# Two scores and two weighted sums by turns: changing the order of attention matmuls in a two-layer kernel

## The chip, the cores and the metric

The kernel runs on one NeuronCore of a Trainium2 chip. The metric is device time in microseconds (us) of one execution. Before the change it is 3041.32 us, the median of three runs (3039.63 to 3041.74). One further execution was recorded by the hardware profiler; its span is 3042.2 us. Engine names are those of the profile: PE is the matmul engine (PEld its weight loads), ACT the scalar engine (exponentials, copies), DVE the vector engine, POOL the GpSimd engine, SP the engine that issues most DMAs. A trailing q (ACTq, SPq) is the queue on which an engine issues DMAs.

## The reference, cut to what matters

The input is `x` of shape (8, 512, 32, 32): eight images, 512 channels, 1024 positions. Two layers follow each other.

```python
# layer 0: 8 heads of 64 channels
h   = group_norm(xf, gn_w, gn_b)
qkv = einsum('oc,bct->bot', qkv_w, h) + qkv_b
q, k, v = split(qkv per head)
q, k, v = fake_quant(q), fake_quant(k), fake_quant(v)   # range over ALL images: a barrier
w   = softmax(einsum('bct,bcs->bts', q*scale, k*scale))
a   = einsum('bts,bcs->bct', w, v)
x   = xf + einsum('oc,bct->bot', proj_w, a) + proj_b
# layer 1: one head of 512 channels
h   = group_norm(x)
q, k, v = h@wq + bq, h@wk + bk, h@wv + bv
x   = x + (softmax(q k^T / sqrt(512)) v) @ wp + bp
```

`fake_quant` takes one minimum and maximum over all images, so all of q, k and v must be computed before any attention of layer 0 may begin. Layer 1's softmax is over one head with 512 channels; its matrices can be combined ("folded") ahead of time: wq with wk into `wa`, wv with wp into `wm`, and the biases likewise.

## The kernel before

It has two phases. Phase 1 (to about 700 us in the profile) normalizes, computes q, k, v of all images and writes them to device memory. Phase 2 runs layer 0's attention for one image while layer 1 works on the image before it. All matmuls pass through one helper, `mm` (line 93), which fixes their order on PE to the order in which the program emits them; other engines' instructions may be put in another order by the framework.

**Attention** is a Python generator over units. A unit is one step of 128 keys for a pair of heads and 512 queries: image b, pair j, half hf, step s; 8 x 4 x 2 x 8 = 512 units. A *burst* is one step of the generator and handles four units; eight units make a *group* (b, j, hf), which is finished by its row sums.

```python
def pair_ps(name):  return ps_s.tile([P, 2, 512], F32, tag="s")   # 2 buffers of two PSUM banks: st
def av_bank(name):  return ps_v.tile([P, 512], F32, tag="v")      # 2 buffers: av
def bank(name):     return ps_o.tile([P, 512], F32, tag="o")      # 2 buffers: everything else

def scores(u):                       # bf16, contraction over 64: both heads of the pair
    st = pair_ps(...)
    for i, r in enumerate(HALF):
        mm(st[:, i, :], lhsT=kt[r, bass.ts(s, P)], rhs=qt[r, bass.ts(hf, 512)], ...)
    pt = ptp.tile([P, 2, 512], F32, tag="p")        # 6 buffers
    nc.scalar.activation(pt, st, AF.Exp, scale=esc)
    ...                                             # s >= 1: DVE adds pt to acc (row sums)

def weighted(u):                     # fp32, two heads side by side in the output's partitions
    if s == 0:
        avs[b, j, hf] = av_bank(...)
    for i, r in enumerate(HALF):
        mm(avs[b, j, hf][r, :], lhsT=pairs[b, j][2][:, s, r], rhs=pt[:, i, :], ...)

def finish(b, j, hf):
    sm = bank(...)
    for i, r in enumerate(HALF):
        mm(sm[r, :], lhsT=ones[:, 0:CH], rhs=acc[:, i, :], start=True, stop=True)
    rs = accp.tile([P, 512], F32, tag="rs")
    nc.scalar.copy(rs, sm)
    inverse(rs, 2, n * 8, rs_d[n], nm)              # 1 / row sums, via device memory
    ao[b, j, hf] = aop.tile([P, 512], F32, tag="ao")
    nc.vector.scalar_tensor_tensor(ao[b, j, hf], avs.pop((b, j, hf)), scl[:, 2:3], rs, ALU.mult, ALU.mult)

for u in range(0, len(units), 4):    # one burst
    ...                              # at hf == 0 and s == 4: load_pair of the next pair
    more = u + 4 < len(units)
    if more:
        scores(u + 4); scores(u + 5)
    for v in range(u, u + 4):
        weighted(v)
    if s == 0 and u > 0:
        finish(*units[u - NT][:3])
    if more:
        scores(u + 6); scores(u + 7)
    yield 6.0 + (s == 0), b
```

When two bursts follow each other with nothing between them, the last two scores of the one and the first two of the next make four scores in a row. `inverse` spreads a row of sums over partitions, takes the reciprocal and broadcasts it back:

```python
def inverse(rs, n_rows, at, scratch, nm):
    k = 4 * n_rows
    group = P // n_rows
    s8 = small.tile([P, 8], F32, tag="s8")[:, 0:k]
    for i in range(n_rows):
        nc.scalar.dma_start(s8[i * group : (i + 1) * group, :],
                            rs[i * group : i * group + 1, :].rearrange("o (p k) -> o p k", k=k))
    r8 = rcs[:, at : at + k]
    nc.vector.reciprocal(r8, s8)
    nc.sync.dma_start(scratch.rearrange("r (p k) -> (r p) k", k=k), r8)
    for i in range(n_rows):
        nc.sync.dma_start(rs[i * group : (i + 1) * group, :],
                          scratch[i : i + 1, :].partition_broadcast(group))
```

**Other work** (fold, projection `pj`, layer 1's `g`, `v2ps`, `s`, `o`) is cut into pieces of four fp32 matmuls (`yield 4.0`; each appears as two instructions in the profile) and interleaved with the bursts by a counter:

```python
F_FIRST = 8.0
folded = 0.0
for w in fold():                     # 8 pieces of 4 matmuls, then 2 bias sums of 8 matmuls each
    folded += w
    while pos < (folded - F_FIRST) * A_IMAGE / F_FOLD:
        advance()                    # one burst
while done < 1:                      # the rest of the first image: burst after burst
    advance()
...
def layer1(b, xt, steps):            # steps: the group norm, in three parts
    for gap, _ in zip(GN_GAPS, steps):   # GN_GAPS = (6.0, 3.0, 3.0)
        yield -gap                   # attention bursts, until gap is filled
```

The group norm makes two tiny matmuls (`gps`, 4 columns); around them, in each of the three gaps, one burst is run.

Of the kernel before, what the change touches and what calls it, by code (L numbers as in the profile page):

```python
# [16 lines left out]
P = 128  # L17
B, C, HH, WW = 8, 512, 32, 32
T = HH * WW
CC = C // P  # L20
NT = T // P
# [25 lines left out]
def attn_pair_kernel(  # L47
# [51 lines left out]
    def norm_steps(src, dst, wcol, bank, nm):  # L99

        st = small.tile([P, CC, NH, 6], F32, tag="gst", name=f"gst_{nm}")
        mv = small.tile([P, CC, 2], F32, tag="gmv", name=f"gmv_{nm}")
        for cc in range(CC):
            for hf in range(NH):
                nc.vector.bn_stats(st[:, cc, hf, :], src(cc, hf))
            nc.vector.bn_aggr(mv[:, cc, :], st[:, cc, :, :].rearrange("p a s -> p (a s)"))
        yield
        ps = bank(f"gps_{nm}")
        mm(ps[:, 0:CC], lhsT=gavg, rhs=mv[:, :, 0], start=True, stop=True)
        mean = small.tile([P, CC], F32, tag="gmean", name=f"gmean_{nm}")  # L110
        nc.vector.tensor_copy(mean, ps[:, 0:CC])  # L111

        d = small.tile([P, CC], F32, tag="gd", name=f"gd_{nm}")
        nc.vector.tensor_sub(d, mv[:, :, 0], mean)
        nc.vector.tensor_mul(d, d, d)
        nc.vector.tensor_add(d, d, mv[:, :, 1])
        yield
        ps2 = bank(f"gps2_{nm}")
        mm(ps2[:, 0:CC], lhsT=gavg, rhs=d, start=True, stop=True)
        rstd = small.tile([P, CC], F32, tag="grstd", name=f"grstd_{nm}")  # L120
        nc.vector.tensor_scalar(rstd, ps2[:, 0:CC], EPS, None, ALU.add)
        nc.gpsimd.tensor_tensor(rstd, rstd, mhalf, ALU.pow)
        nc.vector.tensor_mul(rstd, rstd, vec[:, wcol : wcol + CC])
        for hf in range(NH):
            for cc in range(CC):
                nc.vector.tensor_scalar(  # L126
                    dst(cc, hf), src(cc, hf), mean[:, cc : cc + 1], rstd[:, cc : cc + 1],
                    ALU.subtract, ALU.mult,
                )
        yield  # L130
# [20 lines left out]
    with ExitStack() as fast:  # L151
# [41 lines left out]
        def row_sums(ps, terms):  # L193


            n = len(terms) * CC
            for i, (w, wide) in enumerate(terms):
                for e in range(CC):
                    mm(
                        ps, lhsT=wide[:, e, :], rhs=w[:, e, :],  # L200
                        start=(i == 0 and e == 0), stop=(i * CC + e == n - 1),
                    )

        def widen(dst, col):
            for e in range(CC):
# [10 lines left out]
        with tc.tile_pool(name="p1w", bufs=1) as p1w, tc.tile_pool(name="p1", bufs=2) as p1, tc.tile_pool(  # L216
# [37 lines left out]
            def bias(i):  # L254

                ps = bank(f"bias{i}")
                row_sums(ps, ((wqkv[:, :, bass.ts(i, C)], gbb),))
                if i == 2:
                    nc.vector.tensor_add(vb, vb, ps)  # L259
                    return  # L260
                b4 = qkb[:, bass.ts(i, PAIRS)]
                by_channel(b4, ps)
                nc.vector.tensor_add(
                    b4, b4, vec[:, V_QKB + i * PAIRS : V_QKB + (i + 1) * PAIRS]
                )
# [102 lines left out]
        def inverse(rs, n_rows, at, scratch, nm):  # L368


            k = 4 * n_rows
            group = P // n_rows
            s8 = small.tile([P, 8], F32, tag="s8", name=f"s8_{nm}")[:, 0:k]
            for i in range(n_rows):
                nc.scalar.dma_start(  # L375
                    s8[i * group : (i + 1) * group, :],
                    rs[i * group : i * group + 1, :].rearrange("o (p k) -> o p k", k=k),
                )
            r8 = rcs[:, at : at + k]
            nc.vector.reciprocal(r8, s8)  # L380
            nc.sync.dma_start(scratch.rearrange("r (p k) -> (r p) k", k=k), r8)
            for i in range(n_rows):
                nc.sync.dma_start(
                    rs[i * group : (i + 1) * group, :],
                    scratch[i : i + 1, :].partition_broadcast(group),
                )
# [20 lines left out]
        def attention():  # L407

            units = [(b, j, hf, s) for b in range(B) for j in range(PAIRS) for hf in range(NH)
                     for s in range(NT)]
            pairs = {(0, 0): load_pair(0, 0)}
            pts, accs, avs, sums = {}, {}, {}, []

            def scores(u):
                b, j, hf, s = units[u]
                nm = f"{b}_{j}_{hf}"
                qt, kt, _ = pairs[b, j]  # L420
                st = pair_ps(f"st_{nm}_{s}")
                for i, r in enumerate(HALF):
                    mm(
                        st[:, i, :], lhsT=kt[r, bass.ts(s, P)],
                        rhs=qt[r, bass.ts(hf, 512)], start=True, stop=True,
                    )
                pt = ptp.tile([P, 2, 512], F32, tag="p", name=f"pt_{nm}_{s}")
                nc.scalar.activation(pt, st, AF.Exp, scale=esc)  # L428
                if s == 1:
                    accs[b, j, hf] = accp.tile([P, 2, 512], F32, tag="acc", name=f"acc_{nm}")  # L430
                    nc.vector.tensor_add(accs[b, j, hf], pts[u - 1], pt)
                elif s > 1:
                    nc.vector.tensor_add(accs[b, j, hf], accs[b, j, hf], pt)  # L433
                pts[u] = pt

            def weighted(u):
                b, j, hf, s = units[u]
                if s == 0:
                    avs[b, j, hf] = av_bank(f"av_{b}_{j}_{hf}")
                pt = pts.pop(u)  # L440
                for i, r in enumerate(HALF):
                    mm(
                        avs[b, j, hf][r, :], lhsT=pairs[b, j][2][:, s, r], rhs=pt[:, i, :],
                        start=(s == 0), stop=(s == NT - 1),
                    )

            def finish(b, j, hf):
                nm = f"{b}_{j}_{hf}"
                acc = accs.pop((b, j, hf))
                sm = bank(f"sm_{nm}")  # L450
                for i, r in enumerate(HALF):
                    mm(sm[r, :], lhsT=ones[:, 0:CH], rhs=acc[:, i, :], start=True, stop=True)
                rs = accp.tile([P, 512], F32, tag="rs", name=f"rs_{nm}")
                nc.scalar.copy(rs, sm)
                n = (b * PAIRS + j) * NH + hf
                inverse(rs, 2, n * 8, rs_d[n], nm)
                ao[b, j, hf] = aop.tile([P, 512], F32, tag="ao", name=f"ao_{nm}")
                nc.vector.scalar_tensor_tensor(  # L458
                    ao[b, j, hf], avs.pop((b, j, hf)), scl[:, 2:3], rs, ALU.mult, ALU.mult
                )  # L460

            scores(0)
            scores(1)
            yield 0.0, 0
            scores(2)
            scores(3)
            for u in range(0, len(units), 4):
                b, j, hf, s = units[u]
                if hf == 0 and s == 4:
                    n = b * PAIRS + j + 1  # L470
                    if n < B * PAIRS:
                        pairs[divmod(n, PAIRS)] = load_pair(*divmod(n, PAIRS))


                more = u + 4 < len(units)
                if more:
                    scores(u + 4)
                    scores(u + 5)
                for v in range(u, u + 4):
                    weighted(v)  # L480
                if s == 0 and u > 0:
                    finish(*units[u - NT][:3])
                if more:
                    scores(u + 6)
                    scores(u + 7)
                yield 6.0 + (s == 0), b
            finish(*units[-1][:3])
            yield 1.0, B
# [52 lines left out]
        def layer1(b, xt, steps):  # L541

            for gap, _ in zip(GN_GAPS, steps):
                yield -gap
            hn = hns.pop(b)
            nxt = ahead = None
            vt = l1p.tile([P, NT, C], F32, tag="v", name=f"v2_{b}")
# [76 lines left out]
        def fold():  # L626
# [14 lines left out]
                widen(wide[:, i], col)  # L641
            for i, (dst, w, w2) in enumerate(((gb, wa, wn[NK1]), (ob, wm, wn[WP1]))):
                ps = bank(f"fold_b{i}")
                row_sums(ps, ((w, wide[:, 0]), (w2, wide[:, 1 + i])))
                by_channel(dst, ps)
                yield 8.0
            nc.vector.tensor_add(ob, ob, vec[:, V_BP : V_BP + CC])

        def check_sums():
# [15 lines left out]
        A_IMAGE = PAIRS * NH * (NT * 1.5 + 1.0)  # L665
        F_IMAGE = 4.0 * (8 + 8 + 8 + 16 + 16)
        F_FOLD = 4.0 * (8 + 4)
        F_FIRST = 8.0
        pos, done = 0.0, 0

        def advance():
            nonlocal pos, done
# [18 lines left out]
                advance()  # L691
        while done < 1:
            advance()
        start, other = pos, 0.0
        for w in others():
            until = pos - w
# [369 lines left out]
```

## Time and profile before

| what | value |
|---|---|
| time, median of 3 | 3041.32 us |
| span of the profiled execution | 3042.2 us |
| mean granted PE clock | 0.994 |
| PE / DVE / ACT busy | 2971.1 / 1454.5 / 709.1 us |
| first score of the attention | 705.33 us |
| last piece of fold work ends | about 808 us |
| first projection piece | 856.47 us |

How to read it: busy times are sums over an engine's instructions, and idle time counts only on the engine that sets the end. A wait in the profile is named "engine, what it was about to do <- what released it". The granted clock is the share of full speed that PE's clock was given in a stretch; a mean below 1 means that some stretches ran at half speed, and in those PE counts as busy. Timeline lines give the start, the duration, the engine, line, operation, output <- input, count, and in brackets the idle time before it and its releaser. PE's `st` is a score, `av` a weighted sum, `sm` a row sum, `pt` the exponential of a score, `ao` the finished attention output.

### The profile page before, as it was taken

The page shows a single profiled execution, that of the slowest core. Times are in us where ns is not written, and L with a number is a line of the kernel's source. Part 1 is how long each engine was busy: PE and PEld are TensorE (multiplying, and loading weights), DVE is VectorE, ACT ScalarE, POOL GpSimd, SP SyncE. Part 2 cuts the span into 40 slices and gives each one's busy share as a digit, 9 for nine tenths or more (in the row PEclk, how much of TensorE's full clock was granted, in tenths as well). Part 3 has the DMA queues.
Part 4 walks back from the last instruction along what each step waited for, and adds up shares of the span by engine and source line. Part 5 has one row for each costly group of instructions (what it writes and reads, how often), then busy time and mean ns, then how long its engine had stood idle before and what let it go on. Part 6 is the DMA issues. An engine that isn't in the chain of part 4 may idle for free.

```text
span 3042.2 us, 22770 instructions
## 1 busy us (share of the span) xinstructions
PE 2971.1 (98%) x8664; PEld 1193.5 (39%) x8664; DVE 1454.5 (48%) x2017; ACT 709.1 (23%) x793; POOL 18.5 (1%) x28
## 2 busy tenths in 40 slices
PE   7999999999899999999999999999999999999999
PEld 3444444443233333433333333333333433333443
DVE  6555554447664446344534544364446345533311
ACT  0000000004542333232333223332333233232001
POOL 0000000000000000000000000000000000000000
PEclk9999999999999999999999999999999999999999
DMA  6222222113110111021101101110111012000000
GB/s 252 104 104 104 104 104 81 76 76 128 56 56 28 60 43 63 10 73 63 35 25 63 59 28 50 41 59 28 59 49 63 21 59 61 13 20 23 21 14 22
DMA packets 123287, 182.83 MB, mean 60 GB/s; under 512 B 32800, under 2 KB 65568, under 8 KB 122528
## 3 DMA queue, kind: packets, MB, share of 16 engines
q1 hardware_dynamic: 110336, 180.69, 17.2%
q10 hardware_dynamic: 12832, 0.59, 0.3%
q8 instruction: 70, 1.15, 0.2%
q14 instruction: 49, 0.40, 0.0%
HBM read 113.53 MB, written 67.40 MB: 59 GB/s over the span
## 4 chain that ended last, share of the span: by engine, by line
PE 96%; ACT 1%; issue 1%; DMA 1%; DVE 0%; ACTq 0%; SPq 0%; POOL 0%; POOLq 0%; DVEq 0%
PE av L93 16%; PE s L93 15%; PE o L93 15%; PE qkps L93 15%; PE pj L93 7%; PE g L93 7%; PE v2ps L93 7%; PE vps L93 7%; PE st L93 4%; PE sm L93 2%; ACT pt L428 1%; PE fold L93 1%; PE fold_b L93 0%; PE bias L93 0%; ACTq L375 0%
## 5 line engine op out<-in xcount | busy, mean ns | idle before, releaser
L428 ACT ACTIVATE pt<-st,esc 128x1024 f32<-128x1024 f32 x512 | 547.0, 1114 | 700.9 <-PE st L93 684.3
L433 DVE TENSOR_TENSOR acc<-acc,pt 128x1024 f32<-128x1024 f32 x384 | 469.6, 1223 | 252.5 <-ACT pt L428 233.9
L93 PE MATMUL av<-pt,v 128*64 128x512 f32 x2048 | 483.9, 616 | 3.1 <-DVE ao L458 3.1
L93 PE MATMUL o<-p,v 128*128 128x512 f32 x1024 | 452.4, 595 | 0.7 <-DVE gmean_b L111 0.7
L93 PE MATMUL s<-g,h 128*128 128x512 f32 x1024 | 450.3, 596 | 0.0
L93 PE MATMUL qkps<-h,wqkv 128*128 128x512 f32 x1024 | 447.2, 596 | 2.2 <-DVE h L126 2.2
L93 PEld LDWEIGHTS qkps<-h,wqkv 128*128 128x128 f32 x1024 | 194.4, 191 | 241.9 <-issue 235.9
L93 PEld LDWEIGHTS o<-p,v 128*128 128x128 f32 x1024 | 192.1, 190 | 243.7 <-issue 241.6
L93 PEld LDWEIGHTS s<-g,h 128*128 128x128 f32 x1024 | 191.7, 190 | 243.8 <-issue 243.0
L93 PEld LDWEIGHTS av<-pt,v 128*64 128x64 f32 x2048 | 139.4, 140 | 285.2 <-issue 279.4
L93 PE MATMUL pj<-ao,wp 128*128 128x512 f32 x512 | 225.1, 595 | 0.0
L93 PE MATMUL g<-h,wa 128*128 128x512 f32 x512 | 224.9, 595 | 0.0
L93 PE MATMUL v2ps<-wm,h 128*128 128x512 f32 x512 | 222.9, 593 | 0.0
L93 PE MATMUL vps<-wqkv,h 128*128 128x512 f32 x512 | 221.3, 592 | 0.8 <-DVE vb L259 0.8
L93 PE MATMUL st<-q,k 64*128 64x512 bf16 x1024 | 160.1, 382 | 42.5 <-ACT pt L428 42.5
L296 DVE TENSOR_SCALAR_CACHE_REDUCE qk<-qkps,qkb 128x1024 f32<-128x1024 f32 x64 | 82.2, 1284 | 217.4 <-PE qkps L93 217.3
L637 ACT COPY wa<-fold 128x512 f32<-128x512 f32 x4 | 2.3, 586 | 703.0 <-PE fold L93 703.0
L583 ACT ACTIVATE p<-s 128x512 f32<-128x512 f32 x128 | 76.5, 597 | 361.0 <-PE s L93 361.0
L571 DVE COPY v<-v2ps 128x512 f32<-128x512 f32 x64 | 43.9, 686 | 224.2 <-PE v2ps L93 224.2
L587 DVE TENSOR_TENSOR acc<-acc,p 128x512 f32<-128x512 f32 x96 | 66.2, 689 | 169.1 <-ACT p L583 168.8
L93 PEld LDWEIGHTS vps<-wqkv,h 128*128 128x128 f32 x512 | 97.2, 190 | 123.6 <-issue 122.0
L93 PEld LDWEIGHTS v2ps<-wm,h 128*128 128x128 f32 x512 | 96.7, 190 | 122.1 <-issue 122.1
(112 smaller groups left out, 1386.3 us busy)
## 6 DMA issues: line engine op xcount, KB each, us to landing
x<-in_x_dram SPq DMA_DIRECT2D x32, 512.0 KB, 5.4
q_d<-qk SPq DMA_DIRECT2D x32, 512.0 KB, 2.6
raw<-q_d SPq DMA_DIRECT2D x32, 512.0 KB, 3.4
k_d<-qk SPq DMA_DIRECT2D x32, 512.0 KB, 2.6
raw<-k_d SPq DMA_DIRECT2D x32, 512.0 KB, 4.3
v_d<-v SPq DMA_DIRECT2D x64, 256.0 KB, 2.0
raw<-v_d SPq DMA_DIRECT2D x32, 512.0 KB, 4.2
x<-in_x_dram SPq DMA_DIRECT2D x64, 256.0 KB, 2.6
```

The source lines that it names most:

```text
L93: ins = nc.tensor.matmul(*args, **kw).ins
L296: nc.vector.tensor_scalar(qk, ps.rearrange("p a n -> p (a n)"), qkb[:, t : t + 1], None, ALU.add, ALU.max, accum_out=mx[:, g : g + 1],)
L428: nc.scalar.activation(pt, st, AF.Exp, scale=esc)
L433: nc.vector.tensor_add(accs[b, j, hf], accs[b, j, hf], pt)
L571: nc.vector.tensor_copy(vt[:, t, :], ps)
L583: nc.scalar.activation(pt, ps, AF.Exp, scale=SM1)
L587: nc.vector.tensor_add(acc, acc, pt)
L637: nc.scalar.copy(dst[:, e, :], ps)
```

## The change

It has five parts. Where bursts follow each other (a new flag `dense`: from the start of folding to the end of the first image, and in the gaps of layer 1's group norm), a burst is emitted as two scores, two weighted sums, two scores, two weighted sums, with `finish` last. It is meant to give each exponential the time of two weighted sums before its buffer is needed again. The sums of the folded biases are emitted in pieces of four matmuls instead of eight, so that bursts can come between, and attention starts one piece later (`F_FIRST` 12). The row sums are spread by one DMA on SP's queue, which also carries the loads, instead of one per row on ACT's queue. In the group norm the difference from the mean is taken from PSUM directly, ahead of the copy of the mean.

```diff
@@ norm_steps
-        nc.vector.tensor_copy(mean, ps[:, 0:CC])
-        d = small.tile([P, CC], F32, tag="gd", name=f"gd_{nm}")
-        nc.vector.tensor_sub(d, mv[:, :, 0], mean)
+        d = small.tile([P, CC], F32, tag="gd", name=f"gd_{nm}")
+        nc.vector.tensor_sub(d, mv[:, :, 0], ps[:, 0:CC])
+        nc.vector.tensor_copy(mean, ps[:, 0:CC])
@@ row_sums: after each term's four matmuls
+                yield 4.0
@@ inverse
-            for i in range(n_rows):
-                nc.scalar.dma_start(
-                    s8[i * group : (i + 1) * group, :],
-                    rs[i * group : i * group + 1, :].rearrange("o (p k) -> o p k", k=k),
-                )
+            nc.sync.dma_start(s8, rs[0:P:group, :].rearrange("r (p k) -> r p k", k=k))
@@ attention, one burst
-                more = u + 4 < len(units)
-                if more:
+                if u + 4 < len(units):
                     scores(u + 4)
                     scores(u + 5)
-                for v in range(u, u + 4):
-                    weighted(v)
-                if s == 0 and u > 0:
-                    finish(*units[u - NT][:3])
-                if more:
+                weighted(u)
+                weighted(u + 1)
+                if not dense:
+                    weighted(u + 2)
+                    weighted(u + 3)
+                    if s == 0 and u > 0:
+                        finish(*units[u - NT][:3])
+                if u + 4 < len(units):
                     scores(u + 6)
                     scores(u + 7)
+                if dense:
+                    weighted(u + 2)
+                    weighted(u + 3)
+                    if s == 0 and u > 0:
+                        finish(*units[u - NT][:3])
@@ layer1
+            nonlocal dense
+            dense = True
             for gap, _ in zip(GN_GAPS, steps):
                 yield -gap
+            dense = False
@@ fold
-                row_sums(ps, ((w, wide[:, 0]), (w2, wide[:, 1 + i])))
+                yield from row_sums(ps, ((w, wide[:, 0]), (w2, wide[:, 1 + i])))
                 by_channel(dst, ps)
-                yield 8.0
@@ the counter
-        F_FIRST = 8.0
+        F_FIRST = 12.0
+        dense = True          # set False when the first image is done
```

(Cut: the phase 1 caller of `row_sums` runs it to its end at once, as before.)

More of the change, by code (lines that the diff above doesn't have):

```diff
@@ L256, in bias @@
                 ps = bank(f"bias{i}")
-                row_sums(ps, ((wqkv[:, :, bass.ts(i, C)], gbb),))
+                for _ in row_sums(ps, ((wqkv[:, :, bass.ts(i, C)], gbb),)):
+                    pass
                 if i == 2:
@@ L693, in attn_pair_kernel @@
             advance()
+        dense = False
         start, other = pos, 0.0
```

## The prediction

> **What bounds the kernel now.** I read the page's first part, then the waits of the matmul engine, then its busy time by stretches of 100 us, and last the timeline where those stretches are not full.
>
> ```profile
> PE 2971.1 (98%) x8664; PEld 1193.5 (39%) x8664; DVE 1454.5 (48%) x2017; ACT 709.1 (23%) x793; POOL 18.5 (1%) x28
> ...
> PE 96%; ACT 1%; issue 1%; DMA 1%; DVE 0%; ACTq 0%; SPq 0%; POOL 0%; POOLq 0%; DVEq 0%
> ```
>
> TensorE (PE) is busy 98% of the span and makes up 96% of the chain that ended last. The change removes no matmul, so it can only win what PE loses: idle time and slow clock. The waits of PE (us in total, times, longest) say what it is idle for:
>
> ```profile
> PE st L93 <- ACT pt L428: 42.5, 52, 1.2
> PE gps_a L93 <- POOL gavg L82: 13.9, 1, 13.9
> PE av L93 <- DVE ao L458: 3.1, 4, 1.5
> ```
>
> The 13.9 us are the start and are untouched. The 42.5 us are scores that wait for an exponential to free their accumulator: there are two buffers `st`, and where four scores come in a row the third and fourth wait. Busy time by stretches (the column after POOL is the granted clock) shows where:
>
> ```profile
> 700.00:800.00 100.00, 88.81 (x355) 29.09 (x355) 70.03 (x80) 54.03 (x57) 0.00 (x0) 0.98 0.33 106
> 800.00:900.00 100.00, 86.88 (x333) 28.43 (x330) 69.19 (x83) 47.47 (x48) 0.00 (x0) 0.95 0.20 61
> 900.00:1000.00 100.00, 96.96 (x289) 38.09 (x288) 44.65 (x65) 27.80 (x31) 1.06 (x1) 0.97 0.08 24
> 1000.00:1100.00 100.00, 100.00 (x316) 38.32 (x316) 45.98 (x54) 34.33 (x39) 0.00 (x0) 1.00 0.20 63
> ```
>
> From 700 to 900 us (folding and the first image's attention) PE is idle 11.19 + 13.12 = 24.3 us, 3.1 of it for `ao`. After that it is idle 3.04 us at each of the seven group norms of layer 1, the GN gaps, where three attention bursts have only tiny matmuls between them: 7 x 3.04 = 21.3. And 24.3 - 3.1 + 21.3 = 42.5, so all of it is located, in exactly the places that the change calls dense.
>
> The timeline of a dense stretch shows the mechanism:
>
> ```profile
> 837.36 1.03 PE L93 MATMUL sm<-acc,ones 128*64 128x512 f32 x4
> 838.32 0.61 PE L93 MATMUL st<-q,k 64*128 64x512 bf16 x4
> ...
> 839.05 1.12 ACTq L375 DMA_DIRECT2D s<-rs  x2
> ...
> 840.09 0.39 PE L93 MATMUL st<-q,k 64*128 64x512 bf16 x2 [1.16 <-ACT pt L428]
> ...
> 841.38 0.39 PE L93 MATMUL st<-q,k 64*128 64x512 bf16 x2 [0.91 <-ACT pt L428]
> 841.71 3.65 PE L93 MATMUL av<-pt,v 128*64 128x512 f32 x16
> ...
> 845.44 1.09 SPq L383 DMA_DIRECT2D rs<-rs_d  x2
> ...
> 849.00 0.75 DVE L458 SCALAR_TENSOR_TENSOR ao<-av,scl,rs 128x512 f32<-128x512 f32 x1 [0.90 <-DMA rs<-rs_d]
> ...
> 849.80 1.98 PE L93 MATMUL av<-pt,v 128*64 128x512 f32 x4 [1.51 <-DVE ao L458]
> ```
>
> Two scores go at once (838.32), the next two wait 1.16 and 0.91 us; then four weighted sums run without a gap. Note the last two lines: a new head group may not start its weighted sums until `ao` of two groups earlier has left the `av` bank, and that `ao` comes 11.4 us after its row sums ended (838.32 to 849.75).
>
> [...] sixteen `av` matmuls take 3.65 us at 841.71 and 5.35 us at 914.58, 1.70 more. [...] here slow stretches follow bursts in which PE was idle 1.3 to 2.1 us in two pieces[...]. [...] the pair of issues at 839.05 takes 1.12 us of ACT's queue. [...]
>
> **The change part by part.**
>
> *Scores two by two.* From the timeline: two scores cost 0.53 us up to the next matmul (838.32-type pairs: 880.49 to 881.02), four weighted sums 3.58 us up to the next score (841.71 to 845.29), of which 0.14 is the changeover (8 pairs at 0.43 are 3.44). Two weighted sums are 1.72. In the new order the third score comes 0.53 + 1.72 + 0.14 = 2.4 us after the first and needs the first's exponential: 0.43 until that starts, 1.11 for it, together 1.54. It no longer waits. The fourth needs the second exponential, which starts about 1.0 us later (4.13 us for four), ends at 2.6 and is wanted at 2.6: at most 0.1 to 0.2 left. Against this stands one more changeover per burst: two half bursts cost 2 x 2.39 = 4.78 us against 0.96 + 3.58 = 4.54, so 0.24 each. Dense bursts are 18 in the first image and 3 x 7 in the gaps.
>
> *GN gaps.* Each saves 3.04 and pays 3 x 0.24 = 0.72: net 2.3. But the vector engine must do its work in less time: between the first statistics matmul (912.20) and the first `g` (929.93) it has some 13.5 us of work (six sums at 1.23 to 1.3, eight `h` at 0.46 to 0.54, two or three quantisations at 0.75, small ones), and the new PE time is 2 x 4.78 + 0.96 + 0.8 = 11.3. I allow 0.7 us of a new wait of `g` for `h`. So 1.6 x 7 = 11 us.
>
> *First image.* The start (two waits of the third to sixth score, 3.0 us in sum) stays, because nothing is there to be weighted. All other score waits go. In their place the chain to `ao` shows. The new order puts the row sums at the end of a burst instead of before its last two scores, and bursts get shorter, so from the row sums to the weighted sums that need the bank there are 4.78 + 0.53 = 5.3 us if no fold or projection piece lies between, 5.3 + 3.7 = 9.0 with one piece (8 matmuls of 0.43 and a changeover), 12.7 with two. The chain is 10.4 us where no pair is loaded (785.96 to 796.40) and 11.4 where two raw loads run beside it. One DMA in place of two saves one issue of 0.56[...]. So 9.8 and 11.2. Going through the emission order by hand, with fold pieces of four matmuls and the later start, groups 3 and 5 wait 0.8 each, group 6 2.2, group 7 4.5, group 8 5.9, group 9 none: 14.2. With the start 3.0, about 2 of leftovers, the unchanged burst after the first projection piece (1.6) and 18 x 0.24 = 4.3, that is 25 against 24.3 now. The waits change their name and keep their size: 0, give or take 5.
>
> *Clock.* The losses of clock in the stretches (1 - clock, times 100 us) are about 2 at 700, 5 at 800, 3 at 900, 2 each at 1200, 1400, 2000 and 2600: some 18 us, ten half-rate windows of 1.7. Four lie in the first image and I expect as many after, since a wait of 4 to 6 us is as bad as two of one. Six lie in GN gaps; there I expect one or two left: 8 us won.
>
> *The rest.* The split bias fold moves no work. The norm's subtraction from the accumulator itself saves a 0.16 us copy on a path that PE waits for once (1.0 us). The sums' transfer leaves ACT's queue; in the mixed stretches PE waits for nothing there.
>
> Sum: 11 + 8 + 0 + 1 = 20 us, so 3021 us.
>
> **Rivals.** (1) *All of it is won*: 42.5 - 3 us of score waits and 17 of clock, at 0.24 x 39 = 9 paid: about 48, 2993 us. For it speaks that ACT needs only 4.13 us per four scores. Against it stands the `ao` line above, which already shows at 5 us more distance. (2) *`ao` becomes the bound of the dense run*: the chain stays at 11.4 or grows[...]. Then the first image is 5 to 10 us slower than now and the gain falls to 10 to 15, 3028 us. (3) *DVE becomes the bound*: a dense burst asks 3.5 sums x 1.27, 1.5 quantisation steps x 0.75 and half an `ao`, near 6 us, of DVE per 4.8 of PE. Six `pt` buffers hide a lag of a few us, so it should show only as `g` waiting for `h`; at 3 us per gap the gaps win nothing, 3035 us.
>
> **Range and chances.** Between the first rival and the third, with most weight on 3010 to 3030: 3005 to 3036 holds it 8 times in 10. Two per cent is 61 us, more than all waits and clock losses that can be removed (42.5 + 3.1 + 17), so faster by over 2% is next to impossible; slower by over 2% would take a new stall in every burst.
>
> **What would show it.** The line of scores waiting for `pt` should fall from 42.5 us to 5 to 10; the line of `av` waiting for `ao` should rise from 3.1 to 10 to 20 us with longest waits of 4 to 6, all between 760 and 860 us; a line of `g` waiting for `h` of up to 10 us may appear; the gaps' stretches should read clock 1.00; `s<-rs` should stand in SP's queue x64. If `av<-ao` stays near 3, the gain is nearer 45 us; if the DMA's landing doubles or scores still wait some 40 us, I was wrong.

## The result and the profile after

The changed kernel takes 3006.89 us (median of 4 runs, 3006.25 to 3008.45) against 3041.53 us before in the same comparison: a ratio of 0.9888, 95% interval 0.9871 to 0.9905. That is 34.6 us; I had predicted 20.

The page's first line and the waits of PE after the change (us in total, times, longest):

```profile
PE 2960.3 (99%) x8664; PEld 1185.7 (39%) x8664; DVE 1453.2 (48%) x2017; ACT 705.9 (23%) x793; POOL 18.5 (1%) x28
```

```profile
PE av L93 <- DVE ao L456: 14.3, 5, 5.5
...
PE st L93 <- ACT pt L426: 4.4, 6, 1.2
```

The 42.5 us of scores waiting for `pt` are down to 4.4, and the wait for `ao` has grown from 3.1 to 14.3. Busy time by stretches (PE, PEld, DVE, ACT, POOL, then the granted clock, the DMA share and GB/s):

```profile
700.00:800.00 100.00, 95.80 (x367) 29.57 (x367) 71.90 (x80) 57.03 (x60) 0.00 (x0) 0.97 0.33 106
800.00:900.00 100.00, 85.49 (x329) 27.48 (x328) 70.29 (x87) 44.84 (x45) 0.00 (x0) 0.97 0.20 59
900.00:1000.00 100.00, 100.00 (x319) 38.69 (x318) 48.07 (x66) 33.72 (x38) 1.06 (x1) 1.00 0.10 32
```

From 700 to 900 us PE is still idle for 18.7 us and the clock still falls (0.97 in both stretches); the stretch from 900 us on, with the first GN gap, is full and at full clock, and so are those with the other six gaps.

The two timelines split the 37.7 us between the profiled spans (3042.2 and 3004.5) in three. The first fold matmul starts at 694.93 before and 692.97 after: 2.0 us. Phase 1 hardly changes, and in the profiles of this study, the experiments included, this start lies anywhere from 692.97 to 695.09, so I don't count those 2.0. From there to the first projection piece it took 161.5 us (to 856.47) and now takes 157.3 (to 850.25): 4.3 us. From there to the end it took 2185.7 and now takes 2154.2: **31.5 us, and all of it, to about 0.2, from the seven GN gaps**. One gap, in PE's timeline after:

```profile
900.72 0.61 PE L93 MATMUL st<-q,k 64*128 64x512 bf16 x4
901.26 1.94 PE L93 MATMUL av<-pt,v 128*64 128x512 f32 x8
903.13 0.61 PE L93 MATMUL st<-q,k 64*128 64x512 bf16 x4
903.66 1.94 PE L93 MATMUL av<-pt,v 128*64 128x512 f32 x8
905.53 0.39 PE L93 MATMUL gps_b<-gmv_b,gavg 128*128 128x4 f32 x2
...
914.77 1.94 PE L93 MATMUL av<-pt,v 128*64 128x512 f32 x8
916.64 0.70 PE L93 MATMUL g<-h,wa 128*128 128x512 f32 x1
```

There is no wait in brackets, and `g` starts as soon as the last weighted sums are through. The gap takes 15.92 us (900.72 to 916.64). The same gap in PE's timeline before:

```profile
907.54 0.61 PE L93 MATMUL st<-q,k 64*128 64x512 bf16 x4
...
913.26 0.39 PE L93 MATMUL st<-q,k 64*128 64x512 bf16 x2 [0.68 <-ACT pt L428]
914.26 0.39 PE L93 MATMUL st<-q,k 64*128 64x512 bf16 x2 [0.61 <-ACT pt L428]
914.58 5.35 PE L93 MATMUL av<-pt,v 128*64 128x512 f32 x16
...
922.49 0.39 PE L93 MATMUL st<-q,k 64*128 64x512 bf16 x2 [0.85 <-ACT pt L428]
923.79 0.39 PE L93 MATMUL st<-q,k 64*128 64x512 bf16 x2 [0.90 <-ACT pt L428]
924.11 5.35 PE L93 MATMUL av<-pt,v 128*64 128x512 f32 x16
...
929.93 1.55 PE L93 MATMUL g<-h,wa 128*128 128x512 f32 x3
```

It took 22.39 us (907.54 to 929.93): 3.04 of waits, twice 1.70 of slow clock, and 15.95 of the same work. The trace has the granted clock at 0.50 from 914.68 to 918.10 and from 924.92 to 928.34, with PE busy throughout; pairs of `av` start 0.85 us apart there, and 0.43 after it. Not every gap loses clock: over all seven it is 21.3 us of waits and six half-rate windows of 1.70, 10.2, together the 31.5.

### The profile page after: what moved, and what is told of

Same layout as the page of the kernel before. It is cut to its first block, busy times and chain, and to the rows that moved or that the text cites. A ratio compares the mean times of both kernels' runs of the same rounds, so it can differ in the third digit from the quotient of the medians.

```text
span 3004.5 us, 22663 instructions
## 1 busy us (share of the span) xinstructions
PE 2960.3 (99%) x8664; PEld 1185.7 (39%) x8664; DVE 1453.2 (48%) x2017; ACT 705.9 (23%) x793; POOL 18.5 (1%) x28
## 4 chain that ended last, share of the span: by engine, by line
PE 97%; DVE 1%; DMA 1%; issue 1%; ACT 0%; POOL 0%; SPq 0%; DVEq 0%; ACTq 0%; POOLq 0%
PE av L93 15%; PE s L93 15%; PE o L93 15%; PE qkps L93 15%; PE pj L93 7%; PE g L93 7%; PE v2ps L93 7%; PE vps L93 7%; PE st L93 4%; PE sm L93 2%; ACT pt L426 0%; PE fold L93 0%; DMA raw<-k_d 0%; PE bias L93 0%; DVE acc L431 0%
## 5 line engine op out<-in xcount | busy, mean ns | idle before, releaser
L93 PE MATMUL av<-pt,v 128*64 128x512 f32 x2048 | 480.9, 605 | 14.3 <-DVE ao L456 14.3
L93 PEld LDWEIGHTS av<-pt,v 128*64 128x64 f32 x2048 | 133.1, 137 | 279.1 <-issue 261.4
L93 PEld LDWEIGHTS g<-h,wa 128*128 128x128 f32 x512 | 96.0, 190 | 124.5 <-issue 116.1
```

What stands on the lines that cost most here:

```text
L93: ins = nc.tensor.matmul(*args, **kw).ins
```

## The experiments

The parts can be taken one by one: the new order in the gaps, the new order in the first image, the transfer of the row sums, the fold's pieces. My theory was that the gaps give nearly everything, and that in the first image the waits for `ao` take the place of the score waits. The rivals: the freed ACT queue made the gain, or the smaller pieces did. The norm's subtraction was not run alone; the one wait of PE that names it (`gps_a` for `gd_a`) went from 1.0 to 0.7 us. A ratio is always to the kernel before on the same chip, with its 95% interval.

**The new order in the gaps only.**

```diff
-        dense = True      # from the start of folding
+        dense = False     # still set True in each gap
```

> The changed kernel with the new order only in the gaps of layer 1's group norm; folding and the first image keep the old order. If the gain comes from the gaps (21.3 us of waits and six half-rate windows of 1.7 us), nearly all of it stays: about 3011 us, scores waiting for pt some 21 us, all before 880 us. If the first image's order was worth as much as the gaps', 3020 or more. If the new order there costs time through the waits for ao, 3004 or less.

Measured: 3010.4 us, ratio 0.9898 (0.9882 to 0.9915). Score waits are 18.1 us, all before 900 us, and `av` waits 2.6 for `ao`; from 900 to 3000 us the clock reads 1.00 in every stretch of 100 us. So the first image's order is worth little. In this profile the part from the first fold matmul to the first projection piece takes 158.2 us, against 157.3 with the new order and 161.5 before: of the 4.3 us won there the order brought 0.9, and the other parts of the change, which this run has too, brought 3.3.

**The new order in the first image only.**

```diff
             nonlocal dense
-            dense = True
+            dense = False     # in the gaps
```

> The new order only in folding and the first image; the gaps keep the old order. If the gaps made the gain: about 3038 us (3006.9 + 31.5), with 21 us of score waits after 900 us and some six half-rate windows there. If the first image's order made it: 3020 or less.

Measured: 3036.34 us, ratio 0.9983 (0.9975 to 0.9991). The two halves, each with the other parts of the change, add up to about the whole: 31 and 5 us of 35. The stretches of the second show the gaps nearly as before:

```profile
900.00:1000.00 100.00, 97.25 (x308) 37.40 (x306) 44.11 (x61) 30.59 (x35) 1.06 (x1) 0.98 0.07 21
...
1100.00:1200.00 100.00, 97.25 (x328) 36.86 (x326) 57.04 (x75) 32.97 (x35) 1.01 (x1) 1.00 0.15 50
```

Both gaps lose 2.75 us of waiting (3.04 before; the transfer accounts for the rest, see the next run), but only the first loses clock. There are five slow windows in the seven gaps here, against six in the kernel before: the same waits do or do not trip the clock. The slow windows of the kernel before lie on a grid: from 700 us to its last 5 us it has ten, each of 3.41 us at a granted clock of 0.50, and their starts (709.88, 815.70, 825.94 and on to 2624.76) are whole multiples of 3.41 us apart. What followed a wait went with where in that grid it fell. Waits of 0.68 and 0.61 us that began 1.31 us after a grid point (912.58) were followed by a slow window, and the same two waits beginning 1.43 us after one (2332.64) were not. Of the fourteen bursts that wait in the seven gaps of that trace, all four whose first wait began 0.86 to 1.31 us after a grid point were followed by a slow window, and of the other ten only two (0.13 and 1.35 us after one). So few bursts suggest that the place counts; they show no rule. Three profiles have the old order in the gaps (before, this one and the next); with four to six slow windows in theirs, some 7 to 10 us of the gain is clock, and how much of it a given run of the old order loses is partly luck.

**The transfer alone**, put into the kernel before (the two ACT DMAs replaced by the one SP DMA, nothing else).

> The kernel before with one change alone: the row sums spread by one DMA on SP's queue. My theory: PE does not wait for that chain but for some 3 us, so 3039 to 3042 us. Rival, that the gain came from ACT's queue being freed of 128 issues or from a shorter chain: 3025 us or less.

Measured: 3038.18 us, ratio 0.9992 (0.9983 to 1.0001): at most a few us. The rival falls, but my "nothing" was not quite right either, as PE's waits show:

```profile
PE st L93 <- ACT pt L424: 38.9, 52, 1.2
```

52 waits as before, but 38.9 us instead of 42.5; 2.0 of the difference lies in the gaps. In the old order the row sums' two issues on ACT's queue came between two exponentials (838.92 and 840.22 in the timeline before, 1.30 us apart where four in a row take 1.0 each), and the next score waited for the later one. The twelve runs reach from 3036.2 us at a mean clock of 0.995 to 3042.6 at 0.992: the clock alone moves this kernel by more than the part does, and the profile is of the fastest run, with four windows in the gaps.

**The transfer back on ACT's queue in the changed kernel.**

> The changed kernel with the row sums spread again by one DMA per row on ACT's queue. The one DMA alone took 3.6 us of score waits out of the kernel before, since its two issues held up an exponential. In the new order exponentials have slack, so that effect is gone; what is left is the chain to ao, longer by one issue of 0.56 us for each of five waits: about 3 us, 3010 us, ao waits 16 to 18. Rival, that behind two loads on SP's queue the transfer is later than on ACT's own: ao waits fall below 13 us and the time to 3005 or less.

Measured: 3014.19 us, ratio 0.9903 (0.9887 to 0.992), some 4 us above the changed kernel by ratio, with intervals that overlap. Its profile agrees in kind: `av` waits 17.0 us for `ao` in place of 14.3, scores 5.9 in place of 4.4, and the clock of 800 to 900 us is 0.93 in place of 0.97. The load queue did not delay the transfer on balance: for the first three groups with loads beside them it landed 3.0, 3.0 and 3.8 us after its issue in the changed kernel, the pair on ACT's queue 4.4, 3.9 and 3.8 after its first issue; with no loads it is 1.9 against 2.3.

**The fold in pieces of eight again.**

> The changed kernel with the bias sums folded in pieces of eight matmuls again and attention starting one piece earlier (F_FIRST 8). If the pieces matter only through the distance they put between row sums and the next use of a bank, two places lose a piece between them and one keeps two: ao waits move by a few us either way, 3004 to 3011 us. If the smaller pieces were a main source: 3015 us or more.

Measured: 3010.71 us, ratio 0.9893 (0.9877 to 0.991), not to be told from the changed kernel; `av` waits 15.4 us for `ao`. So the smaller pieces were no main source; that they matter only through where they fall fits this, but one run does not show it.

**Row sums one burst earlier.** If `ao` is what the first image now waits for, more distance must take the wait away. A group's sums on DVE should be complete by about its last weighted sum, so in the dense order `finish` can follow that sum at once:

```diff
                 if dense:
                     weighted(u + 2)
                     weighted(u + 3)
-                    if s == 0 and u > 0:
-                        finish(*units[u - NT][:3])
+                    if s == 0 and u > 0:
+                        close(units[u - NT][:3])   # finish, if not finished yet
+                    if s == 4:
+                        close(units[u][:3])
```

> The changed kernel with a group's row sums and ao one burst earlier where the order is dense (right after the group's own last weighted sum instead of one burst later). If the distance between row sums and the next use of the av bank sets the 14.3 us that weighted sums wait for ao, they fall below 3 us, two of the four half-rate windows of the first image go with them, and the time is 2988 to 2993 us. Rival, that the vector engine is behind by then: the row sums or the exponentials wait for its sums instead, a new wait of 5 us or more on PE, and 3000 to 3007 us.

Measured: 2990.88 us, ratio 0.983 (0.9814 to 0.9846), 16 us below the changed kernel. Waits of PE and the stretch of 800 to 900 us:

```profile
PE st L93 <- ACT pt L426: 4.6, 6, 1.2
...
PE sm L93 <- DVE acc L431: 1.1, 1, 1.1
```

```profile
800.00:900.00 100.00, 98.30 (x406) 32.01 (x406) 83.00 (x107) 56.26 (x57) 2.09 (x1) 1.00 0.22 69
```

No line of `av` waiting for `ao` is left, and from 800 to 900 us PE goes from 85.49 to 98.30 busy at full clock. From the first fold matmul to the first projection piece it takes 140.1 us in place of 157.3, with 13.0 us of waits and three of four half-rate windows gone, one of these at the start (the clock of the two stretches from 700 us reads 0.98 and 1.00 in place of 0.97 twice). DVE, at 83%, costs 1.1 us once: the rival holds in kind, not in size.

**The new order everywhere.**

```diff
-            dense = False     # after the gaps, and after the first image
```

> The changed kernel with the new order in every burst, also where other work lies between bursts. My prediction charged 0.24 us per burst for one more changeover between scores and weighted sums; 89 more bursts would then cost 21 us, 3028 us. What the gaps showed (they gained waits and clock in full) says that the changeover costs nothing: a burst between other work has four changeovers in either order. Then 3005 to 3007 us, with the score waits of the one burst after the first projection piece (1.6 us) gone.

Measured: 3027.45 us, ratio 0.995 (0.9934 to 0.9967), about 19 us slower than the changed kernel by ratio. My expectation fell; the charge of the prediction, 0.24 us a burst, came true in size for bursts between other work, though not for its reason. One such burst in PE's timeline, first of the changed kernel, then of this one:

```profile
974.05 0.61 PE L93 MATMUL st<-q,k 64*128 64x512 bf16 x4
974.59 3.65 PE L93 MATMUL av<-pt,v 128*64 128x512 f32 x16
978.18 0.60 PE L93 MATMUL st<-q,k 64*128 64x512 bf16 x4
978.71 6.71 PE L93 MATMUL s<-g,h 128*128 128x512 f32 x15
```

```profile
975.65 0.60 PE L93 MATMUL st<-q,k 64*128 64x512 bf16 x4
976.18 1.94 PE L93 MATMUL av<-pt,v 128*64 128x512 f32 x8
978.05 0.75 PE L93 MATMUL st<-q,k 64*128 64x512 bf16 x4
978.73 1.94 PE L93 MATMUL av<-pt,v 128*64 128x512 f32 x8
980.60 4.99 PE L93 MATMUL s<-g,h 128*128 128x512 f32 x11
```

From the first score to layer 1's next matmul it takes 4.66 us in the old order and 4.95 in the new: the switch from weighted sums to layer 1's full-width matmuls costs as much (eight `av` take 1.72 of the 1.87 us up to the next start) as the switch to a score, so the half bursts do have one switch more, five against four. That is half of the 0.29 us. The other half is a short wait inside the second pair of scores, which takes 0.68 us up to the next start in place of 0.53: its later score starts at 978.41, and the exponential that frees its buffer ended at 978.36. Over 89 bursts the measured 19 us, and the 1.6 us of waits gained after the first projection piece, make 0.23 each. In the profile such short waits come to 6.6 us, in 40 of the bursts; the remaining 14 or so are the extra switch, 0.15 to 0.16 each.

**All three ideas together, first with the new order everywhere**: early row sums, and the first four scores in two pairs with fold pieces between them and before the first burst.

> Row sums one burst earlier, the new order everywhere, and the first four scores spread over two fold pieces (two before the fourth piece, two before the fifth, bursts after that). Against the version with early row sums (2990.9 us): 1.6 us of score waits after the first projection piece and 2.8 at the start go, and the half-rate window at the start may: 2984 to 2988 us, score waits below 1 us. Rival: with five or more bursts in a row at the end of the first image the vector engine falls behind, and row sums wait for acc by 3 us or more: 2990 us.

Measured: 3011.0 us, ratio 0.9892 (0.9875 to 0.9908). The waits did go: no line of scores waiting for `pt` is left, and the first image runs at full clock (1.00 in both stretches from 700 to 900 us). What it wins is taken back by the mixed bursts (those between other work), with their changeovers and short waits, and `o` now waits 4.8 us for the copy of row sums. Both expectations missed that: they took the new order to be free in mixed bursts.

**The same with the new order only where bursts follow each other**, and in the burst after the first projection piece:

```diff
         scores(2); scores(3)
+        yield 0.0, 0
...
-        F_FIRST = 12.0
+        F_FIRST = 16.0
...
             folded += w
+            if folded in (12.0, 16.0):
+                advance()          # two scores each
...
-        dense = False              # at the end of the first image
+            if n_piece == 0:       # after the bursts of the first projection piece
+                dense = False
```

> Early row sums, the first four scores spread over two fold pieces, and the new order only where bursts follow each other, including the burst after the first projection piece. If a half burst's extra changeover (0.24 us, 89 bursts, 21 us) is what made the run with the new order everywhere slow, this gets the rest of its gains without that price: score waits near 0, no half-rate window in the first image, 2984 to 2988 us. If something else made that run slow, it stays above 2990 us.

Measured: **2984.36 us**, ratio 0.9816 (0.9799 to 0.9832), faster than both kernels. PE's waits and the stretches:

```profile
PE av L93 <- DVE ao L456: 1.1, 1, 1.1
...
PE sm L93 <- DVE acc L431: 0.7, 1, 0.7
```

```profile
700.00:800.00 100.00, 99.27 (x393) 31.60 (x393) 74.00 (x90) 59.70 (x63) 0.00 (x0) 1.00 0.35 111
800.00:900.00 100.00, 98.87 (x402) 32.20 (x401) 85.41 (x110) 56.89 (x58) 2.09 (x1) 1.00 0.23 70
```

No line of scores waiting for `pt` is left, and 1.9 us of other waits remain in the two stretches that once lost 24.3. Apart from the start (14.3 us), the waits of PE in the whole span come to 7.0 us. From the first projection piece on this run takes 2153.1 us; the one before it, which differs in the order of the mixed bursts alone, takes 2179.7.

## Why the prediction was right, and where its sum was off

**Right: where the idle time lay and what takes its place.** Scores waiting for `pt` were to fall to 5 to 10 us; they fell to 4.4, which is the start (2.8, in four waits and not two) and the burst after the first projection piece (1.6). The "about 2 of leftovers" came as pairs of scores of about 0.75 in place of 0.60 us, seven of them, about 1 us in sum.

**Right in kind, and in sum nearly to the figure: the chain to `ao`.** The prediction walked through the order by hand and gave the groups 0.8, 0.8, 2.2, 4.5 and 5.9 us, 14.2 in sum. Measured, in the same order: 0.78, 0.66, 3.01, 4.44 and 5.45, sum 14.3. That the sums agree so well is partly luck, as the third wait came out 0.8 longer and the fifth 0.45 shorter. The two longest, in PE's timeline:

```profile
825.94 3.63 PE L93 MATMUL av<-pt,v 128*64 128x512 f32 x8 [4.44 <-DVE ao L456]
...
843.79 3.27 PE L93 MATMUL av<-pt,v 128*64 128x512 f32 x8 [5.45 <-DVE ao L456]
```

Eight `av` that should take 1.94 take 3.63 and 3.27: each of these two waits brings its slow window with it, as expected (granted clock 0.50 for 3.41 us from 826.04 and from 843.11); the wait of 3.01 us brought none. The chain itself was put at 9.8 and 11.2 us, the second with an allowance of mine for the loads that no trace had shown; it measures 10.0 (row sums' end at 815.92 to 825.89) and 11.0 (832.76 to 843.74). But the loads did not set the difference between the two, as the prediction had it. The broadcast sums of both groups landed 9.0 us after the row sums (at 824.88 and 841.81); then the first `ao` came 0.3 us later and the second 1.2, each behind a sum that the vector engine had in hand. The run with early row sums shows that more distance takes the waits away.

**Mis-sized: "So 1.6 x 7 = 11 us" for the gaps.** The term came to 21.3. Two deductions in it were not paid. The 0.7 us for `g` waiting for `h` does not exist after. The prediction counted all 13.5 us of the vector engine's work ahead of the first `g`; in the trace it is busy 9.85 of the 11.11 us from the first statistics matmul to `g`, and half of the eight `h` come only after `g` has started (916.64; the last `h` ends at 919.37). And the 0.72 for three changeovers is not an extra in a gap. The 0.24 for one compared two half bursts (4.78) with a burst whose four scores come in a row (0.96 + 3.58). Where something else parts the scores, the old burst is 2 x 0.53 + 3.58 = 4.64, which leaves 0.14, as in the mixed bursts. In a gap the old order paid even that in another coin, since its waits made it issue two scores singly (0.39 and 0.32 us at 913.26 and 914.26, 0.53 for a pair). 15.95 and 15.92 us of work per gap are the measurement.

**Mis-sized: the clock.** One or two windows were to stay in the gaps; none did, 10 us in place of 8. That six stood there to be won was itself partly luck, since the profiles with the same old order in the gaps have four to six.

**Mis-sized: "0, give or take 5" for the first image.** It won 4.3 us, within the margin. The new order had only 0.9 of them by the run with the old order there. The transfer alone takes 1.5 (161.5 to 160.0 in its profile), and for the first image the prediction had counted nothing for it beyond the shorter chain to `ao`.

**The range, and a sum that does not hold.** All these terms erred to the same side, so the result lies only 1.9 us above the lower end of 3005 to 3036. Nor are 61 us "more than all waits and clock losses that can be removed": 42.5 + 3.1 + 17 is 62.6. The last experiment won 57 of them.

**The rivals of the prediction.** "All of it is won" is what the gaps did and the first image did not. "`ao` becomes the bound" is true of the first image, though the transfer in the load queue was not the reason: beside loads it landed 3.0 to 3.8 us after its issue, the pair on ACT's queue 3.8 to 4.4. "DVE becomes the bound" is not seen as `g` waiting for `h`, but DVE has a part in the waits for `ao`. For the two longest, the reciprocal started 1.3 and 0.2 us after its data had landed and `ao` 0.3 and 1.2 after its own, each time behind another instruction on DVE: some 1.5 us of each chain. With `ao` out of the way DVE, at 83 to 85%, costs about 1 us.

## What to carry to other kernels

When an engine waits for a buffer because its instructions come in bunches, emit them so that the releasing engine gets its time from work in between; but look first for the next wait on the same path, and shorten or advance that chain in the same step (here its distance was worth 16 us, nearly half of what the change itself brought). Reorder only where the wait is: the same order in bursts that never waited cost 19 us. And short idle spells cost twice where they trip the clock (1.29 us of waits and 1.70 of slow clock in the burst that first waits at 912.58), which here hung on when they fell.

## What the runs showed of the hardware that I had not expected

A switch between matmuls of different kinds has a price on PE of 0.08 to 0.15 us in these traces: 64-row bf16 scores to fp32 weighted sums 0.08 (0.53 us for two scores that start 0.22 to 0.23 apart), back 0.14 (3.58 for 3.44), and from the paired 64-column weighted sums to full-width fp32 matmuls 0.15 (1.87 for 1.72). Eight of the ten half-rate windows of the kernel before (granted clock 0.50, 3.41 us each) followed bursts with only 1.3 to 2.1 us of idle time in two pieces, while one wait of 3.01 us in the changed kernel was followed by none; length alone did not decide, since the same waits of 0.68 and 0.61 us were followed by a window when they began 1.31 us into the grid of 3.41 us, and by none at 1.43. And issuing two DMAs on ACT's queue put 1.30 us between two exponentials that otherwise start 1.0 apart (838.92 and 840.22, then 841.23 and 842.23).
